# Gated attention with a mixture of experts on one core: when the values' banks are emptied, when Wk is turned, and where the sums for keys and values are made

## The chip, the cores and the metric

The kernel runs on one core of a Trainium2 chip. The core has TensorE (PE, matrix products), VectorE (DVE), ScalarE (ACT), GpSimd (POOL) and SyncE (SP, here only a queue that issues transfers). Each engine works off its own list of instructions in order; semaphores tie the lists together. The metric is the device time of one execution in microseconds, as the median of three runs.

## The reference

The input is `x`, 2 batches of 1024 tokens, 512 wide, all in float32. With `xn` the layer norm of `x`, the result is

```
qkv = xn @ w_qkv.T + b_qkv ;  q, k, v = split(qkv)
s   = softmax(q k' / sqrt(512)) v @ w_out.T + b_out
full_w = softmax weights of the 2 best of 8 experts, from xn @ router_w + router_b
f   = sum over experts e of full_w[e] * silu(xn @ expert_w[e] + expert_b[e])
y   = xn + f @ proj_w + proj_b
g   = silu(norm_w * y / rms(y))
out = x + s * g
```

## The kernel before, in words

The 2048 tokens are 16 tiles of 128 (`NT`). The kernel folds weights: the value and output weights become one matrix `rwvo`, the query and key weights one matrix `wqk`. So there is one product for the values and one for the queries, and the keys are the transposed tokens `xnT` themselves. The stages are:

1. **Weights** (to about 24 us): Wv, Wo and Wq are loaded; `wZ` is the buffer from which `turn_w` (line 132 on) transposes Wq, and later Wk, on DVE.
2. **Layer norm and values** (24 to 92 us, loop over `t` at line 442): `norm(g)` handles tiles 2g and 2g+1 in three parts. `stats` computes mean and variance on DVE and the root on ACT. `shifts` makes scale and shift on DVE. `rows` applies them on ACT, writes the tile to DRAM (`xn_d`), and, for tiles from 4 on, writes it a second time in blocks (`xn_s`) and reads it back (`xz`), from where `turn_x` transposes it on DVE into `xnT`. Tiles 0 to 3 are transposed on PE and copied by DVE (line 378). Each iteration multiplies one tile by `rwvo` (line 457) into a PSUM tile `pv` of the pool `ps_big`, which has two such tiles. ACT then copies the values to `vo` (line 465) and DVE adds the router's bias to the logits `lg1` (line 466). Only after both may the products of tile t+2 write that PSUM tile. Between the tiles lie the transposition of Wk, two weighted column sums (`sk`, `vb`), and at `t == 12` the load of all expert weights.
3. **Routing, queries and experts** (92 to 256 us): the tokens' order by expert, the product `wqk`, the queries of batch 0, and 39 blocks of expert products with their gathers. PE works there without a break.
4. **Attention** (256 us to the end), in pairs of tiles. The first pair's scores are made directly (`scores`, line 996). All later pairs use a scheme of Strassen and Winograd with 7 in place of 8 block products: `pair_scores` (line 1015) for scores, `attend` (line 1086) for probabilities times values. It needs sums of blocks of the right-hand factor, once for each batch: `right_sums` (line 866) makes t2, t3, t4 and overwrites block b12 by b12 - b11. `sum_right` makes them from the keys `xnT` on DVE, `sum_values` from the values `vo` on POOL, there in two halves for each sum. `sum_left` and `sum_p` make the sums for the left-hand factors on POOL. For each pair the expert outputs are gathered (`fetch`), scaled (ACT), combined (DVE), written to DRAM and read back in blocks (`cs`, `cz`), transposed (`turn_c`) and projected; `add_b` adds the projection's bias to the residual row `xr` on POOL. The probabilities take the same way through DRAM (`ps`, `pz`, `turn_p`).

What sets the order is the order in which the code is written: `keep_order` ties every instruction behind the one written before it for the same engine. So a step that waits holds up all that is written after it for that engine. The SP queue, too, takes its transfers strictly in that order, and each waits for the data that it moves and for the buffer that it fills. The part of the attention stage that precedes its loop is this, with the first batch's sums:

```
keys = sum_right(0)
next(keys)
sum_left(1)
both_of(fetch, 0)
sum_values(0)
scores(0)
...
*_, tw[0] = keys
```

`right_sums` is a generator: each `next` issues one sum. A product of pair 1 reads t2 first, then t3, b12, t4.

Of the kernel before, what the change touches and what calls it, by code (L numbers as in the profile page):

```python
# [14 lines left out]
ALU = mybir.AluOpType  # L15
# [5 lines left out]
P = 128  # L21
# [6 lines left out]
def kernel(  # L28
# [332 lines left out]
    def norm(g):  # L361
        stats(g)
        shifts(g)
        rows(g)
# [71 lines left out]
    direct(2)  # L436
    direct(3)
    norm(2)
    rows(1)


    for t in range(NT):
        if t % 2 == 0 and 0 < t and t + 6 < NT:
            norm(t // 2 + 3)
        if 3 < t < NT - 2:
            turn_x(t + 2)
        pv = ps_big.tile([P, 2, 512], FP, tag="big", name=f"pv{t}")
        for n, cols in ((1, ds(HH + E1, HH)), (0, ds(0, HH + E1))):
            if n == 0 and t in (1, 2):
                turn_x(t + 1)  # L450
            if n == 0 and t == 1:
                norm(3)
            if n == 0 and t == 3:
                turn_x(4)
                turn_x(5)
            for c in range(KC):
                pe.matmul(  # L457
                    pv[:, n, : HH + E1 * (1 - n)],
                    lhsT=xnT[t // ST][:, c, ts(t % ST, P)],
                    rhs=rwvo[:, c, cols],  # L460
                    start=(c == 0),
                    stop=(c == KC - 1),
                )
        dst = vo[t // ST][:, t % ST, :].rearrange("p (n f) -> p n f", n=2)
        act.copy(dst, pv[:, :, 0:HH])
        dve.tensor_tensor(lg1[:, t, :], pv[:, 0, HH : HH + E1], rb, ALU.add)
        if t == 1:
            spread(sp, wZ[1], w_qkvT[:, ts(1, H)])
        if t == 2:
            gps.dma_start(bo, b_out.partition_broadcast(P))  # L470
        if t == 4:
            turn_w(wqkT[:, KC:], wZ[1])
        if t == 6:
            sk_ = weighted(wqkT[:, KC:], bqk[:, 0], "sk")
        if t == 8:

            vb = weighted(wo, bqkv[:, 2], "vb")
        if t == 9:
            dve.tensor_copy(u, columns(sk_, "pu"))
        if t == 11:  # L480
            pvb = ps_mm.tile([P, 512], FP, tag="mm", name="pvb")
            pe.matmul(pvb, lhsT=ones, rhs=vb, start=True, stop=True)
            dve.tensor_tensor(bo, pvb, bo, ALU.add)
            close(raw_guard)
            ew_guard, ewp = pool("ew", side="right")
            ew = ewp.tile([P, E, KC, H], FP, name="ew")
        if t == 12:
            for e in range(E):
                sp.dma_start(ew[:, e], expert_w[e].rearrange("(c p) f -> p c f", p=P))
    close(ln_guard)  # L490
    eb_guard, ebp = pool("eb", side="right")
    eb = ebp.tile([P, E, H], FP, name="eb")
# [373 lines left out]
    def right_sums(b_, w_, eng, parts):  # L866

        b11, b12, b21, b22 = b_
        t2, t3, t4 = (w_[:, i] for i in range(3))
        def less(dst, l_, r_):  # L870
            for n in range(parts):
                c = ts(n, l_.shape[1] // parts)
                eng.tensor_tensor(dst[:, c], l_[:, c], r_[:, c], ALU.subtract)  # L873

        less(t3, b22, b12)
        yield
        less(b12, b12, b11)
        yield
        less(t2, b22, b12)
        yield  # L880
        less(t4, b21, t2)
        yield b12, t2, t3, t4

    def sum_right(b):
# [6 lines left out]
    def sum_values(b):  # L891
        if b == 0:
            w_ = at.tile([P, 3, SK, HH], FP, name="tv", bufs=1)
        else:

            w_ = keys_at[0][:, : 3 * SK * HH].rearrange("p (i k f) -> p i k f", i=3, k=SK)
        *_, tv[b] = right_sums(values(b), w_, gps, 2)

    def sum_p(k):

# [165 lines left out]
    def attend(k):  # L1066
# [53 lines left out]
        plus(c12, p5, c12)  # L1120
        yield
        p4 = times(a22, t4, ps_s, "s")
        finish(1, ds(HH, HH))
        plus(c21, p4, c21)
        yield
        if not last:
            plus(c12, times(s4, b22, ps_mm, "mm"), c12)
            for i in (1, 0):
                gate(rows[i], rows[i], two[i], ds(0, H))
                gps.tensor_tensor(rows[i], rows[i], base[two[i]], ALU.add)  # L1130
                sp.dma_start(out_d[:, two[i], :], rows[i])
        else:

            parts = [times(s4, b22[:, :, ts(n, P)], ps_mm, "mm") for n in range(2)]
            finish(1, ds(0, HH))
            finish(0, ds(HH, HH), store=False)
            for n in range(2):
                cols = ds(HH + n * P, P)
                gate(parts[n], parts[n], two[0], cols)
                plus(rows[0][:, cols], parts[n], rows[0][:, cols])  # L1140
                sp.dma_start(out_d[:, two[0], cols], rows[0][:, cols])
# [5 lines left out]
                step(t)  # L1147


    keys = sum_right(0)  # L1150
    next(keys)
    sum_left(1)
    both_of(fetch, 0)
    sum_values(0)
    scores(0)
    take_p(0)
    scores(1)
    close(ps_guard)
    ps_guard, ps_s = pool("ps_s", bufs=4, space=PSUM)
    *_, tw[0] = keys  # L1160
    both_of(scale_c, 0)
    both_of(inverse, 0)
    take_p(1)
    sp.dma_start(pb, proj_b.partition_broadcast(P))
    both_of(fetch_x, 0)
    both_of(combine, 0)
    both_of(take_c, 0)
    sp.dma_start(nw, norm_w.partition_broadcast(P))
    both_of(add_b, 0)
    both_of(fetch, 1)  # L1170
    queries_of(0, lambda name: ps_mm.tile([P, 512], FP, tag="mm", name=name))
    for k in range(NP):
        more = k + 1 < NP
        final = k + 2 == NP
        if more:
            n = pair_scores(k + 1)
            next(n)
            if k:
                both_of(scale_c, k + 1)
                both_of(turn_c, k)  # L1180
            if k + 1 == NPB:
                sum_values(1)
# [115 lines left out]
```

## Time and profile before

| what | value |
|---|---|
| median of three runs | 547.65 us (546.2, 547.65, 547.86) |
| the profiled execution's own time | 545.15 us |
| its span, first to last instruction | 543.5 us |
| PE busy | 527.6 us, 97% of the span |
| DVE busy | 315.8 us, 58% |
| ACT busy | 156.9 us, 29% |
| POOL busy | 225.0 us, 41% |
| mean granted clock of PE | 0.994 of full speed |
| the chain that ended last | PE 81%, DVE 8%, DMA 5% |

An instruction line of a timeline gives the start and the busy time in us, the engine, the line of the kernel, the operation, what is written and read, the shape, the count of instructions merged into it, and in brackets the idle time of the engine before it and what ended that. The line of a window gives its bounds and length, then busy time and count for PE, PE's weight loads, DVE, ACT and POOL, then PE's granted clock, the share of the transfer engines in use, and the rate in GB/s. The chain of waits gives start, duration and what the time was spent on, followed back from the last instruction to what released each one. PE's busy time counts a matmul as pipelined, so two neighbours overlap in it; the distance between starts is the true pace.

### The profile page before, as it was taken

The page shows a single profiled execution, that of the slowest core. Times are in us where ns is not written, and L with a number is a line of the kernel's source. Part 1 is how long each engine was busy: PE and PEld are TensorE (multiplying, and loading weights), DVE is VectorE, ACT ScalarE, POOL GpSimd, SP SyncE. Part 2 cuts the span into 40 slices and gives each one's busy share as a digit, 9 for nine tenths or more (in the row PEclk, how much of TensorE's full clock was granted, in tenths as well). Part 3 has the DMA queues.
Part 4 walks back from the last instruction along what each step waited for, and adds up shares of the span by engine and source line. Part 5 has one row for each costly group of instructions (what it writes and reads, how often), then busy time and mean ns, then how long its engine had stood idle before and what let it go on. Part 6 is the DMA issues. An engine that isn't in the chain of part 4 may idle for free.

```text
span 543.5 us, 5795 instructions
## 1 busy us (share of the span) xinstructions
PE 527.6 (97%) x1754; PEld 321.4 (59%) x1754; DVE 315.8 (58%) x525; ACT 156.9 (29%) x259; POOL 225.0 (41%) x239
## 2 busy tenths in 40 slices
PE   8969999999999999999989999999999999999996
PEld 7848787444444444444456666656756657484486
DVE  3645852831333333335498468376597685949686
ACT  3353322111211111112332522422425234152330
POOL 5000000023354863200777444346279855464542
PEclk9998999999999999999989999999999999999999
DMA  9879859839999999994556912822724728285512
GB/s 249 234 257 286 274 180 382 327 82 315 284 307 334 344 320 305 303 272 151 184 203 193 326 65 79 306 72 97 258 77 148 253 81 292 77 302 189 190 56 79
DMA packets 90928, 118.66 MB, mean 218 GB/s; under 512 B 6928, under 2 KB 55184, under 8 KB 90768
## 3 DMA queue, kind: packets, MB, share of 16 engines
q1 hardware_dynamic: 79344, 89.16, 51.1%
q0 software_dynamic: 5792, 18.88, 10.9%
q10 hardware_dynamic: 5760, 10.23, 5.0%
q8 instruction: 15, 0.25, 0.2%
q14 instruction: 17, 0.14, 0.1%
HBM read 73.69 MB, written 44.56 MB: 218 GB/s over the span
## 4 chain that ended last, share of the span: by engine, by line
PE 81%; DVE 8%; DMA 5%; issue 3%; ACT 1%; SPq 1%; DVEq 0%; ACTq 0%
PE ph L759 20%; PE so L1086 17%; PE pp L1015 14%; PE po L952 10%; PE pv L457 6%; PE pq L500 5%; PE pr L519 3%; PE sc L996 3%; PE pqk L531 3%; DMA wZ<-in_L_attn_w_qkv_dram 2%; DVE xnT L873 1%; DMA xn_d<-xn 1%; DMA xn_s<-xn 1%; DMA wo<-in_L_attn_w_out_dram 1%; DVE sc L1021 1%
## 5 line engine op out<-in xcount | busy, mean ns | idle before, releaser
L759 PE MATMUL ph<-ew,gT 128*128 x280 | 120.3, 592 | 0.0
L733 POOL DMA_INDIRECT xg<-xn_d,tok x39 | 37.3, 956 | 163.6 <-DVE npast L678 103.6
L759 PEld LDWEIGHTS ph<-ew,gT 128*128 128x128 f32 x280 | 53.2, 190 | 67.0 <-issue 67.0
L785 DVE TENSOR_TENSOR h<-ph,eb 128x512 f32<-128x512 f32 x39 | 26.8, 688 | 80.9 <-issue 53.1
L457 PE MATMUL pv<-rwvo,xnT 128*128 128x256 f32 (+1 forms) x256 | 60.2, 393 | 5.6 <-DVE xnT L378 5.0
L457 PEld LDWEIGHTS pv<-rwvo,xnT 128*128 128x128 f32 x256 | 48.9, 194 | 15.8 <-issue 4.2
L788 ACT ACTIVATE h<-h 128x512 f32<-128x512 f32 x39 | 24.6, 632 | 96.2 <-DVE h L785 87.8
L952 PE MATMUL po<-pw,ct 128*128 128x512 f32 x112 | 49.2, 592 | 0.0
L983 ACT ACTIVATE pr<-sc,nm 128x1024 f32<-128x1024 f32 x16 | 18.3, 1145 | 95.1 <-DVE nm L980 93.4
L1093 DVE TENSOR_TENSOR o<-so,o 128x256 f32<-128x256 f32 x49 | 20.0, 420 | 39.1 <-PE so L1086 22.2
L1130 POOL TENSOR_TENSOR o<-o,base 128x512 f32<-128x512 f32 x14 | 20.6, 1492 | 49.1 <-DVE o L1096 48.1
L1015 PE MATMUL pp<-xnT,qT 128*128 128x512 f32 x84 | 39.5, 592 | 0.0
L1086 PE MATMUL so<-vo,pT 128*128 128x256 f32 x168 | 38.5, 379 | 0.0
L952 PEld LDWEIGHTS po<-pw,ct 128*128 128x128 f32 x112 | 21.3, 190 | 25.5 <-issue 25.3
L1086 PEld LDWEIGHTS so<-vo,pT 128*128 128x128 f32 x168 | 31.9, 190 | 7.3 <-issue 2.6
L914 POOL DMA_INDIRECT hg<-ho_d,posi_m x32 | 31.4, 982 | 10.7 <-issue 6.7
L1021 DVE TENSOR_TENSOR sc<-pp,sc 128x512 f32<-128x512 f32 x49 | 31.6, 677 | 4.2 <-PE pp L1015 4.2
L120 DVE STREAM_TRANSPOSE gT<-sz 128x512 f32<-128x512 f32 x39 | 27.3, 700 | 7.3 <-DMA sz<-xs 7.3
L519 PE MATMUL pr<-xnT,wqk 128*128 128x256 f32 x128 | 28.8, 381 | 0.9 <-DVE sc L1021 0.9
L1015 PE MATMUL pp<-tw,sw 128*128 128x512 f32 x56 | 26.8, 623 | 2.5 <-DVE tw L873 2.5
L120 DVE STREAM_TRANSPOSE pT<-pz 128x1024 f32<-128x1024 f32 x14 | 28.1, 2008 | 0.0
L500 PE MATMUL pq<-xnT,wqk 128*128 128x512 f32 x64 | 28.1, 594 | 0.0
(210 smaller groups left out, 780.0 us busy)
## 6 DMA issues: line engine op xcount, KB each, us to landing
xs<-xg SPq DMA_DIRECT2D x39, 256.0 KB
sz<-xs SPq DMA_DIRECT2D x39, 256.0 KB
ho_d<-h ACTq DMA_DIRECT2D x39, 256.0 KB
ew<-in_L_ffn_expert_w_dram SPq DMA_DIRECT2D x8, 1024.0 KB
ps<-pr SPq DMA_DIRECT2D x16, 512.0 KB
pz<-ps SPq DMA_DIRECT2D x16, 512.0 KB
x<-_attn_hidden_states_dram SPq DMA_DIRECT2D x16, 256.0 KB
xn_d<-xn SPq DMA_DIRECT2D x16, 256.0 KB
```

Source lines behind the costliest of these rows:

```text
L120: dve.transpose(dst.rearrange(f"p j {order} -> p i j a", a=QP), z.rearrange("p i (j b) -> p i j b", b=QP),)
L457: pe.matmul(pv[:, n, : HH + E1 * (1 - n)], lhsT=xnT[t // ST][:, c, ts(t % ST, P)], rhs=rwvo[:, c, cols], start=(c == 0), stop=(c == KC - 1),)
L500: pe.matmul(ps[:, half, :], lhsT=wqk[:, c, ts(oc, P)], rhs=xnT[0][:, c, ts(half, 512)], start=(c == 0), stop=(c == KC - 1),)
L519: pe.matmul(ps[:, :PW], lhsT=wqk[:, c, ts(oc, P)], rhs=xnT[1][:, c, ts(k, PW)], start=(c == 0), stop=(c == KC - 1),)
L733: gps.indirect_dma_start(out=xg[s], out_offset=None, in_=xn_d, in_offset=bass.IndirectOffsetOnAxis(ap=tok[:, s : s + 1], axis=0),)
L759: pe.matmul(ph, lhsT=g_[:, c, :], rhs=ew[:, ds(r, 1), c, :].rearrange("p e f -> p (e f)"), start=(c == 0), stop=(c == KC - 1),)
L785: dve.tensor_tensor(h, ph, eb[:, ds(r, 1), :].rearrange("p e f -> p (e f)"), ALU.add)
L914: gps.indirect_dma_start(out=g_, out_offset=None, in_=ho_d, in_offset=bass.IndirectOffsetOnAxis(ap=posi_m[:, n, t : t + 1], axis=0),)
L952: pe.matmul(po, lhsT=c_[:, c, :], rhs=pw[:, c, :], start=(c == 0), stop=(c == KC - 1))
L1015: pe.matmul(ps, lhsT=l_[:, c, :], rhs=r_[:, c, :], start=(c == 0), stop=(c == KH - 1))
L1021: dve.tensor_tensor(dst, ps, other, ALU.add)
L1086: pe.matmul(ps[:, :w_], lhsT=l_[:, c, :], rhs=r_[:, c, :], start=(c == 0), stop=(c == SK - 1),)
```

## The change

In the layer-norm loop a tile's products (`value_side`) and the emptying of its PSUM tile (`keep_values`) become two functions, and iteration t empties tile t-1 after it has issued tile t's products. The layer norms of later tiles (`norm`, and `rows(1)`, which stood ahead of the loop) are written behind that, no longer ahead of the products. Wk's load goes from `t == 1` to `t == 4`, behind the transfers of tiles 10 and 11 in the SP queue, and its transposition from `t == 4` to `t == 8`; the sums that follow move by one to three iterations, and the closing of the buffers goes from `t == 11` to `t == 12`.

In `right_sums` t2 is now made as t3 + b11 in place of (b12 - b11) subtracted from b22, so t3, t2 and t4 all read only unchanged blocks, and b12 is overwritten last. The first batch's value sums are made on DVE, whole and not in halves (4 in place of 8 instructions); the second batch's stay on POOL. Ahead of the attention loop the sums are spread: two key sums before the first scores, one key sum and three value sums between the two scores, the overwriting of the keys' block behind the second softmax, and that of the values' block behind `combine`. The loads of `pb`, `xr` and `nw` and the `add_b` of the first pair go ahead of the scores, and the write of the combined rows goes ahead of the second read of probabilities. In the last `attend`, one `finish` moves ahead by one product.

```diff
-    rows(1)
...
     for t in range(NT):
-        if t % 2 == 0 and 0 < t and t + 6 < NT:
-            norm(t // 2 + 3)
         if 3 < t < NT - 2:
             turn_x(t + 2)
-        pv = ps_big.tile([P, 2, 512], FP, tag="big", name=f"pv{t}")
-        for n, cols in ((1, ds(HH + E1, HH)), (0, ds(0, HH + E1))):
-            if n == 0 and t in (1, 2):
-                turn_x(t + 1)
-            if n == 0 and t == 1:
-                norm(3)
-            if n == 0 and t == 3:
-                turn_x(4)
-                turn_x(5)
...
-        dst = vo[t // ST][:, t % ST, :].rearrange("p (n f) -> p n f", n=2)
-        act.copy(dst, pv[:, :, 0:HH])
-        dve.tensor_tensor(lg1[:, t, :], pv[:, 0, HH : HH + E1], rb, ALU.add)
+        value_side(t)
+        if t:
+            keep_values(t - 1)
         if t == 1:
-            spread(sp, wZ[1], w_qkvT[:, ts(1, H)])
+            rows(1)
+            norm(3)
+        if t == 3:
+            turn_x(4)
+            turn_x(5)
+        if t % 2 == 0 and 0 < t and t + 6 < NT:
+            norm(t // 2 + 3)
         if t == 2:
             gps.dma_start(bo, b_out.partition_broadcast(P))
         if t == 4:
+            spread(sp, wZ[1], w_qkvT[:, ts(1, H)])
+        if t == 8:
             turn_w(wqkT[:, KC:], wZ[1])
-        if t == 6:
+        if t == 9:
             sk_ = weighted(wqkT[:, KC:], bqk[:, 0], "sk")
-        if t == 8:
+        if t == 10:
             vb = weighted(wo, bqkv[:, 2], "vb")
-        if t == 9:
+        if t == 11:
             dve.tensor_copy(u, columns(sk_, "pu"))
-        if t == 11:
+        if t == 12:
             pvb = ps_mm.tile([P, 512], FP, tag="mm", name="pvb")
...
-        if t == 12:
             for e in range(E):
                 sp.dma_start(ew[:, e], expert_w[e].rearrange("(c p) f -> p c f", p=P))
+    keep_values(NT - 1)
...
         less(t3, b22, b12)
         yield
+        more(t2, t3, b11)
+        yield
+        less(t4, b21, t2)
+        yield
         less(b12, b12, b11)
-        yield
-        less(t2, b22, b12)
-        yield
-        less(t4, b21, t2)
         yield b12, t2, t3, t4
...
             w_ = at.tile([P, 3, SK, HH], FP, name="tv", bufs=1)
-        else:
-            w_ = keys_at[0][:, : 3 * SK * HH].rearrange("p (i k f) -> p i k f", i=3, k=SK)
-        *_, tv[b] = right_sums(values(b), w_, gps, 2)
+            return right_sums(values(b), w_, dve, 1)
+        w_ = keys_at[0][:, : 3 * SK * HH].rearrange("p (i k f) -> p i k f", i=3, k=SK)
+        return right_sums(values(b), w_, gps, 2)
...
         p4 = times(a22, t4, ps_s, "s")
+        finish(0, ds(HH, HH), store=False)
         finish(1, ds(HH, HH))
...
             finish(1, ds(0, HH))
-            finish(0, ds(HH, HH), store=False)
...
-    keys = sum_right(0)
-    next(keys)
+    keys, vals = sum_right(0), sum_values(0)
+    for _ in range(2):
+        next(keys)
     sum_left(1)
     both_of(fetch, 0)
-    sum_values(0)
+    sp.dma_start(pb, proj_b.partition_broadcast(P))
+    both_of(fetch_x, 0)
+    both_of(add_b, 0)
+    sp.dma_start(nw, norm_w.partition_broadcast(P))
     scores(0)
+    next(keys)
+    for _ in range(3):
+        next(vals)
     take_p(0)
     scores(1)
...
-    *_, tw[0] = keys
+    tw[0] = next(keys)
     both_of(scale_c, 0)
     both_of(inverse, 0)
+    both_of(combine, 0)
+    tv[0] = next(vals)
     take_p(1)
-    sp.dma_start(pb, proj_b.partition_broadcast(P))
-    both_of(fetch_x, 0)
-    both_of(combine, 0)
     both_of(take_c, 0)
-    sp.dma_start(nw, norm_w.partition_broadcast(P))
-    both_of(add_b, 0)
     both_of(fetch, 1)
...
             if k + 1 == NPB:
-                sum_values(1)
+                *_, tv[1] = sum_values(1)
```

More of the change, by code (lines that the diff above doesn't have):

```diff
@@ L438, with value_side @@
     norm(2)
-    rows(1)
-    for t in range(NT):
-        if t % 2 == 0 and 0 < t and t + 6 < NT:
-            norm(t // 2 + 3)
-        if 3 < t < NT - 2:
-            turn_x(t + 2)
+    pvs = {}
+    def value_side(t):
         pv = ps_big.tile([P, 2, 512], FP, tag="big", name=f"pv{t}")
+        pvs[t] = pv
         for n, cols in ((1, ds(HH + E1, HH)), (0, ds(0, HH + E1))):
@@ L463, with keep_values @@
                 )
+    def keep_values(t):
+        pv = pvs.pop(t)
         dst = vo[t // ST][:, t % ST, :].rearrange("p (n f) -> p n f", n=2)
@@ L466 @@
         dve.tensor_tensor(lg1[:, t, :], pv[:, 0, HH : HH + E1], rb, ALU.add)
-        if t == 1:
-            spread(sp, wZ[1], w_qkvT[:, ts(1, H)])
+    for t in range(NT):
+        if 3 < t < NT - 2:
+            turn_x(t + 2)
+        value_side(t)
+        if t:
+            keep_values(t - 1)
+        if t == 1:
+            rows(1)
[5 more added lines that the diff above has]
+            norm(t // 2 + 3)
         if t == 2:
@@ L869, in right_sums, with in_parts, less, more @@
         t2, t3, t4 = (w_[:, i] for i in range(3))
-        def less(dst, l_, r_):
+        def in_parts(dst, l_, r_, op):
             for n in range(parts):
                 c = ts(n, l_.shape[1] // parts)
-                eng.tensor_tensor(dst[:, c], l_[:, c], r_[:, c], ALU.subtract)
+                eng.tensor_tensor(dst[:, c], l_[:, c], r_[:, c], op)
+        def less(*which):
+            in_parts(*which, ALU.subtract)
+        def more(*which):
+            in_parts(*which, ALU.add)
         less(t3, b22, b12)
         yield
-        less(b12, b12, b11)
-        yield
-        less(t2, b22, b12)
+        more(t2, t3, b11)
         yield
         less(t4, b21, t2)
+        yield
+        less(b12, b12, b11)
         yield b12, t2, t3, t4
```

## The prediction

> **What bounds the kernel now.** I read the page first, then the chain of waits, then the timelines around each place where TensorE (PE) stands still, last the windows with the granted clock.
>
> ```profile
> PE   8969999999999999999989999999999999999996
> ...
> PEclk9998999999999999999989999999999999999999
> ```
>
> PE is busy 97% of the span. So only its few holes and slow stretches can be won: the 6 of slice 3 (27 to 41 us) and the 8 of slice 21 (272 to 285), with the clock's dips in slices 4 and 21. The chain of waits names what stands before PE there:
>
> ```profile
> 37.00 0.48 ACT vo L465
> ...
> 40.01 0.61 DVE xnT L378
> 40.76 5.45 PE pv L457 x16
> ...
> 77.53 14.06 PE pv L457 x64
> ...
> 271.80 7.96 DVE xnT L873
> ```
>
> A tile of values is 16 PE records. Unhindered it takes 14.06 / 4 = 3.51 us (last line but one); tile 3 took 5.45, 1.94 more. PE's timeline gives the holes:
>
> ```profile
> 33.21 1.97 PE L457 MATMUL pv<-rwvo,xnT 128*128 128x256 f32 x8 [1.67 <-DVE xnT L378]
> 40.76 19.50 PE L457 MATMUL pv<-rwvo,xnT 128*128 128x256 f32 x80 [3.36 <-DVE xnT L378]
> 60.78 7.58 PE L457 MATMUL pv<-rwvo,xnT 128*128 128x256 f32 x32 [0.52 <-DVE lg L466]
> ...
> 276.79 1.88 PE L1015 MATMUL pp<-xnT,qT 128*128 128x512 f32 x4
> 281.16 5.19 PE L1015 MATMUL pp<-tw,sw 128*128 128x512 f32 x8 [2.50 <-DVE tw L873]
> ```
>
> The first number in brackets is the hole. Behind two of them PE is slow, not just late; the windows (length, busy time by engine, then the granted clock) say why:
>
> ```profile
> 31.65:35.06 3.41, 1.85 (x9) 1.61 (x10) 2.33 (x7) 0.91 (x3) 0.00 (x0) 1.00 1.00 284
> 38.48:41.89 3.41, 1.13 (x5) 1.05 (x6) 1.71 (x6) 2.09 (x4) 0.00 (x0) 1.00 1.10 375
> 41.89:45.30 3.41, 3.41 (x9) 2.67 (x9) 2.08 (x3) 0.20 (x1) 0.00 (x0) 0.50 1.04 390
> 277.41:280.82 3.41, 1.25 (x3) 0.19 (x1) 3.38 (x2) 0.64 (x2) 1.26 (x2) 1.00 0.64 214
> 280.82:284.23 3.41, 3.07 (x4) 1.51 (x5) 3.38 (x6) 0.00 (x0) 1.52 (x2) 0.50 0.52 188
> ```
>
> After a window in which PE was busy 1.13 or 1.25 of 3.41 us the next ran at clock 0.50; after one with 1.85 it did not. DMA's share (last but one) is above 1 in the loop: transfers land there in the order of the queue, some 0.7 us apart.
>
> **Rule against row, the clock.** The Trainium skill (TensorE: Matmul & The Clock Gate, "What's actually happening") has the clock halved after an idle window of about 3.4 us. By it the 2.50 us hole costs 2.5. The row has 1.25 us of work in the window before and still 0.50 after: the 24 matmuls of pair 1 after the hole take 293.06 - 281.16 = 11.9 us where 24 x 0.43 = 10.3 would do, so the hole costs 2.5 + 1.6 = 4.1. I take the row, but the windows' place in a run is chance: a 2.5 us hole puts some 1.9 us into one window in about two of three positions.
>
> **The change, part by part: the loop.** Nothing is added; the orders on VectorE (DVE), ScalarE (ACT) and the SP queue move. A tile's bank is now emptied (ACT copy, then DVE's `lg` sum) behind the next tile's products. For even tiles that leaves ACT's order as it was (copy, layer norm's std and two xn, copy, copy); on DVE the transposed tiles now stand one place further ahead of `lg`. I replay it with durations of the trace. The layer-norm chain, from one `lg` (37.51) over statistics, std, shifts, two xn and the next copy to the next `lg` (42.12), is 4.6 us.
> - Tile 2. xn of tiles 2 and 3 (`rows(1)`) go behind copy 0, which runs at 30.3 and not 31.70. DVE's xnT of tile 2 goes before `lg`, done by 30.4. Tile 2 starts when tile 1 ends, 31.4, not 33.21.
> - Tile 3. xnT 3 now stands ahead of tile 4's statistics (done 34.4), which removes the releaser of the 3.36. But copy 1 is behind xn 7, which waits, as before, for a transfer that lands at 36.1 (xn 4's buffer). Copy 1 37.5, `lg` 37.7: start 37.75, not 40.76. This leaves a hole of 2.4, which may halve the clock of tile 3 (end 41.3, or 43.0).
> - Tile 4. Its turn on DVE waits for `lg` of tile 2, 42.3 by the 4.6 chain, plus 0.95: start 43.3 (46.24 before); the slow tile 3 is hidden by that wait.
> - Tile 5. DVE now has turns 5 and 6 ahead of `lg` 3, and turn 6 needs its transfer. The trace's record of landings has it at 46.6, and the SP queue up to there is unchanged. Turn 47.6, `lg` 47.75: start 47.8 (49.75 before), a new hole of 1.0.
> - Tile 6. The chain of 4.6 runs from that `lg`: 52.4 (53.25 before), a hole of 1.1.
> - After that PE is ahead of nothing: per two tiles it needs 7.0 us, the chain less. The four Wk transfers (42.99 to 44.55 issued, last landed 52.6, about 1.2 us each) have left the queue before xn 8's write, so turn 8 has its data at about 51.2 (needed 52.2), and go behind tile 11's; they land at about 61.5. DVE reaches `turn_w` (2.5) at 62.5, then the `sk` and `vb` sums (2.8 each) and three turns without a pause, so `lg` 9 is done at 70.05: 0.25 us of hole at tile 11. The hole of 0.52 and two of 0.27 in tiles 8 to 11 go.
> - End: 52.4 + 10 x 3.51 + 0.25 + two small products of 0.86 = 89.5, where the next product now starts at 91.5. **Gain 2.0**, although holes and slow clock were 8. The 8 MB of expert weights are issued 1.4 us later (79, not 77.56); they end near 110, gathers start near 113.
>
> **Keys and values.** DVE's view of the hole, with GpSimd's (POOL):
>
> ```profile
> 270.08 1.22 DVE L976 TENSOR_REDUCE nm<-sc 128x1 f32<-128x1024 f32 x1 [5.14 <-PE sc L996]
> ...
> 271.72 8.04 DVE L873 TENSOR_TENSOR xnT<-xnT 128x1024 f32<-128x1024 f32 x1
> 279.79 1.23 DVE L873 TENSOR_TENSOR tw<-xnT 128x1024 f32<-128x1024 f32 x1
> ```
>
> ```profile
> 264.10 0.96 POOL L914 DMA_INDIRECT hg<-ho_d,posi_m  x1 [1.01 <-DMA ho_d<-h]
> ...
> 268.82 2.50 POOL L873 TENSOR_TENSOR tv<-vo 128x512 f32<-128x512 f32 x2
> ...
> 276.19 2.48 POOL L873 TENSOR_TENSOR tv<-vo,tv 128x512 f32<-128x512 f32 x2
> ```
>
> An operation of 1.22 us took 8.04: it came to an end only when POOL's eight value sums did (278.67). Then two key sums followed and PE waited. In the change t3, t2 and t4 no longer read the changed block. t3 and t2 (2 x 1.23) fit between 260.49 and the first softmax at 263.21. t4 and three value sums (4 x 1.23 = 4.9) fill DVE's idle 5.14 before 270.08. The changed block comes after the second softmax, 271.8, behind whatever POOL then does. POOL loses eight sums (10 us) and gets `add_b` (1.5 + 1.7) from 269 on; its loads (pb, xr) are issued from about 256, when SP is idle. At worst DVE waits for it till 272.9 and has the block at 274.1. The product that needs it is the fourth of pair 1, at 276.79 + 3 x 1.72 = 281.9. The last value sum and two combines (5 us with contention) end before 280.3, DVE's first sum of pair 1. So the hole goes: pair 1 ends 28 x 0.43 = 12.0 after 276.79, at 288.8 and not 293.06. **Gain 4.2**. Later work follows: turn of the gathered tiles done at 294.5, wanted at 295.7; the sums of p on POOL end at 294, wanted at 302.6. The take of the second p moves behind two cs writes in SP, 277.2 as before.
>
> **Rule against row, the port.** By SBUF — State Buffer, "SBUF: two separate sides", a VectorE operation with two SBUF inputs and a GpSimd one exclude each other for one whole instruction. This speaks against the move: four DVE sums now lie beside the four gathers from 264.10. The 8.04 shows a longer hold, over the rest of a run of POOL instructions. The nearest row the other way round is this pair:
>
> ```profile
> 450.20 1.41 DVE L970 SCALAR_TENSOR_TENSOR y<-y,rrms,nw 128x512 f32<-128x512 f32 x2
> ...
> 450.97 1.46 POOL L914 DMA_INDIRECT hg<-ho_d,posi_m  x1 [0.30 <-issue]
> ```
>
> DVE ran on, the gather took 0.5 more. By that, gathers end about 1 us later; were they held for the whole run (till 269.9), they would end at 273.4 and land near 278, and the combine and last value sum would end at 280.4: 0.1 us of price. I take the row. The other way, DVE held by gathers and `add_b` (till 272), the second softmax would be 5 us late and PE's banks with it: 3 us of hole.
>
> **The rest.** Later batches' sums keep number and engine (POOL, 8 x 1.26, already there); only their order changes: nothing. In the tail one gate and sum (0.9 us) fills DVE's hole of 0.12 before 537.41: 0.1.
>
> **Sum.** 2.0 + 4.2 + 0.1 = 6.3 against the profiled 545.15 (span 543.5): 538.9. The runs' median, 547.65, is 2.5 above that execution. Halved clock behind the keys is met in two of three placements, so I count 1.1 of its 1.6: gain 5.7, **541.9**.
>
> **Rivals.**
> - Loop gives nothing (0.20). The transposed turns now wait in DVE ahead of `lg`; a transfer of tile 6 or 8 two us later shifts tile 6 by as much. For: queue full (share above 1). Against: tile 8's comes earlier. 543.9.
> - Keys give nothing (0.08): DVE held beside gathers and `add_b` as above, a 3 us hole in place of 2.5; 547.65 - 2.1 + 0.5 = 546.0.
> - Loop gives more (0.06): turn 6 has its data at 45.3, as 14 of its 16 parts did; tiles 5 and 6 follow without holes. 540.
> - Slower (0.08): `turn_w` waits in DVE for Wk, moved behind tile 11's transfers, and tile 12's queue behind it. Everything on DVE after 62.5 is late with it, one for one; 64.5 eats the loop's gain, 68.2 all of it. It takes transfers of 2.9 us in place of 1.2. At 71: 550.
> - The forecast (0.58), its own range 540.3 to 543.5.
>
> A measurement of this kernel tells 0.3% (1.6 us) from no change. Faster by more: 0.58 + 0.20 + 0.06 and a little of the second rival, 0.86; within it the rest of that, 0.06; slower 0.08. Range 539.2 to 545.4.
>
> **What would show it.** Right: PE's hole of 2.50 and its 0.50 window near 281 gone, DVE's changed block at 1.2 to 2.5 us; value tiles start near 31.4, 37.8, 43.3, 47.8, 52.4; DVE idle before turn 6 for its transfer. Wrong: a hole of PE in tiles 8 to 12 with DVE waiting for Wk; POOL's gathers stretched past 275; PE waiting for ct at the first projection.

## The result, and the profile after

| | before | after |
|---|---|---|
| median of 13 runs each, us | 546.2 (545.32 to 549.64) | 542.69 (540.4 to 545.93) |
| ratio, 95% interval | | 0.9935 (0.9913 to 0.9957) |
| profiled execution, us | 545.15 | 542.69 |
| its span, us | 543.5 | 541.0 |
| first value product to first `pqk` (the loop), us | 67.61 | 66.65 |
| first scores to first projection `po`, us | 43.83 | 41.69 |
| the rest, to the end | | the same within 0.1 |

The kernel became faster by 3.5 us (2.3 to 4.8 by the interval), 0.65%. The two profiled executions are only 2.46 us apart, and their stages add up: the loop gained 0.96, the keys' stage 2.14, and the loop began 0.67 later (24.49 and not 23.82) in this execution. That start is chance: the five kernels of this study that keep the loop of before, and so are the same up to there, began it between 23.82 and 27.30 us.

The busy share of PE in 40 slices of the span, and its granted clock, on the page of the kernel after:

```profile
PE   8979999999999999999999999999999999999996
...
PEclk9998999999999999999999999999999999999999
...
PE 74%; DMA 10%; DVE 8%; issue 4%; ACT 1%; POOL 1%; SPq 1%; DVEq 0%; POOLq 0%; ACTq 0%
```

The dip in slice 21 is gone, in work and in clock; the one in slices 3 and 4 is smaller, but there. In the chain that ended last (third line) DMA has risen to 10%, from 5%.

In the timeline of PE after, the two stages look like this:

```profile
39.55 5.47 PE L450 MATMUL pv<-rwvo,xnT 128*128 128x256 f32 x16 [3.40 <-DVE lg L462]
45.26 7.45 PE L450 MATMUL pv<-rwvo,xnT 128*128 128x256 f32 x32 [0.23 <-DVE xnT L120]
53.47 14.33 PE L450 MATMUL pv<-rwvo,xnT 128*128 128x256 f32 x64 [0.76 <-DVE lg L462]
...
284.12 1.98 PE L1033 MATMUL pp<-tw,qT 128*128 128x512 f32 x4 [0.60 <-ACT sc L1041]
...
293.98 3.72 PE L531 MATMUL pr<-xnT,wqk 128*128 128x256 f32 x16 [0.91 <-DVE sc L1039]
```

Tile 3 started at 39.55 and not at 37.75, behind a hole of 3.40; 0.67 of the difference is the later start of the loop. In place of the pause of 2.50 there were two, where I had forecast none: one of 0.60 us within pair 1's products and one of 0.91 in the products behind them. Why, the other engines show. VectorE, from the last expert blocks on:

```profile
261.58 0.69 DVE L797 TENSOR_TENSOR h<-ph,eb 128x512 f32<-128x512 f32 x1 [3.02 <-DMA ho_d<-h]
263.57 0.69 DVE L797 TENSOR_TENSOR h<-ph,eb 128x512 f32<-128x512 f32 x1 [1.30 <-DMA ho_d<-h]
264.18 1.22 DVE L885 TENSOR_TENSOR tw<-xnT 128x1024 f32<-128x1024 f32 x1
...
275.97 1.21 DVE L885 TENSOR_TENSOR xnT<-xnT 128x1024 f32<-128x1024 f32 x1
```

The changed block now takes 1.21 us, not 8.04. But the first key sum starts at 264.18, 3.7 us later than before (260.49), because two expert outputs `h` waited 3.02 and 1.30 us for earlier ones to be written out; before, that wait was 0.45. The chain of waits follows the same delay through POOL to the pause of PE:

```profile
256.26 5.20 DMA ho_d<-h
...
262.97 4.40 DMA ho_d<-h
...
267.58 0.73 POOL sw L872
...
278.30 4.56 DMA hg<-ho_d,posi_m
...
283.64 1.22 DVE vo L885
284.86 0.61 DVE sc L1039
```

The query sums start at 267.58 (258.99 before), the last gather at 278.30, and VectorE's first sum of pair 1 at 284.8, where I had put it at 280.3.

### The profile page after: what moved, and what is told of

It reads as the page before. It is cut to its first block, busy times and chain, and to the rows that moved or that the text cites. A ratio compares the mean times of both kernels' runs of the same rounds, so it can differ in the third digit from the quotient of the medians.

```text
span 541.0 us, 5784 instructions
## 1 busy us (share of the span) xinstructions
PE 527.2 (97%) x1754; PEld 320.9 (59%) x1754; DVE 314.9 (58%) x529; ACT 156.9 (29%) x259; POOL 217.7 (40%) x231
## 4 chain that ended last, share of the span: by engine, by line
PE 74%; DMA 10%; DVE 8%; issue 4%; ACT 1%; POOL 1%; SPq 1%; DVEq 0%; POOLq 0%; ACTq 0%
PE ph L771 20%; PE so L1104 17%; PE pp L1033 12%; PE po L970 10%; PE pq L512 5%; PE pv L450 4%; DMA wZ<-in_L_attn_w_qkv_dram 3%; PE pqk L543 3%; DMA xn_s<-xn 2%; PE pr L531 2%; DMA ho_d<-h 2%; DVE sc L1039 1%; DVE pT L120 1%; DMA xn_d<-xn 1%; DMA wo<-in_L_attn_w_out_dram 1%
## 5 line engine op out<-in xcount | busy, mean ns | idle before, releaser
L1001 ACT ACTIVATE pr<-sc,nm 128x1024 f32<-128x1024 f32 x16 | 18.3, 1146 | 89.5 <-DVE nm L998 78.4
L531 PEld LDWEIGHTS pr<-xnT,wqk 128*128 128x128 f32 x128 | 24.0, 190 | 8.1 <-DVE sc L1039 4.2
```

What stands on the lines that cost most here:

```text
L531: pe.matmul(ps[:, :PW], lhsT=wqk[:, c, ts(oc, P)], rhs=xnT[1][:, c, ts(k, PW)], start=(c == 0), stop=(c == KC - 1),)
```

## The experiments

All times are medians of runs beside runs of the kernel before. "Loop" and "keys" are the two distances of the table above, read in the profiled execution.

| kernel | us (runs) | ratio (95%) | loop | keys |
|---|---|---|---|---|
| before | 546.0 to 546.7 | 1 | 67.61 | 43.83 |
| loop alone | 544.6 (22) | 0.9971 (0.9956 to 0.9986) | 66.01 | 44.0 |
| keys alone | 544.1 (22) | 0.9964 (0.9946 to 0.9981) | 67.71 | 40.45 |
| after, loads put back | 540.99 (6) | 0.9906 (0.9878 to 0.9935) | 65.98 | 39.56 |
| before, loads moved | 542.02 (6) | 0.9921 (0.9891 to 0.995) | 68.28 | 39.56 |
| value sums behind the block | 542.32 (8) | 0.9939 (0.992 to 0.9959) | 67.57 | 39.56 |
| value sums whole on POOL | 542.42 (6) | 0.9938 (0.9916 to 0.996) | 67.58 | 39.56 |
| copy first | 540.47 (6) | 0.991 (0.9882 to 0.9939) | 66.27 | 39.57 |
| rows late | 542.22 (7) | 0.9928 (0.9897 to 0.9959) | 66.40 | 39.57 |
| loop, and whole sums | 541.43 (6) | 0.9911 (0.9881 to 0.9941) | 66.42 | 39.57 |
| rows late, Wk later | 537.46 (5) | 0.9854 (0.9834 to 0.9874) | 63.27 | 39.56 |

My theory after the result: the loop and the keys each give what was worked out, and what is missing went to the loads of `pb`, `xr` and `nw`, which now stand ahead of the last `h` writes. The rival: the loads are innocent, and the gathers and value sums hold each other up.

**The loop alone.** All of the change up to the expert stage (its core here), with the keys' part, the loads and the tail as before.

```diff
-        pv = ps_big.tile([P, 2, 512], FP, tag="big", name=f"pv{t}")
...
-        act.copy(dst, pv[:, :, 0:HH])
-        dve.tensor_tensor(lg1[:, t, :], pv[:, 0, HH : HH + E1], rb, ALU.add)
+        value_side(t)
+        if t:
+            keep_values(t - 1)
...
-        if t == 4:
+        if t == 8:
             turn_w(wqkT[:, KC:], wZ[1])
```

> The kernel before with the change's layer-norm loop alone (emptying one tile later, Wk loaded and turned later), keys and values untouched. Theory A (the loop's order is worth something, but each tile still waits for a transfer): value tiles 5 and 6 start some 1 to 2 us earlier than before, 1 us is left at the end of the loop, the hole of 2.5 us before pair 1 stays: 0.5 to 2 us faster than before. Rival (the changed kernel's whole gain lies here, the keys' part gives nothing): 3 to 3.5 us faster. Rival (loop gives nothing): within 0.5 us of before.

Measured 544.6, 1.4 us less by the medians and 1.6 by the ratio, with a loop of 66.01 (1.6 less) and the hole of 2.50 at the keys unchanged. So the loop's part works, at 1.0 to 1.6 us (the four executions with this code took 66.65, 66.01, 65.98 and 66.42) and not 2.0.

**The keys alone.** The keys' and values' sums and the loads as changed (cut here), with the loop and the tail as before.

```diff
+        more(t2, t3, b11)
+        yield
+        less(t4, b21, t2)
+        yield
         less(b12, b12, b11)
...
+            return right_sums(values(b), w_, dve, 1)
...
+    sp.dma_start(pb, proj_b.partition_broadcast(P))
+    both_of(fetch_x, 0)
+    both_of(add_b, 0)
+    sp.dma_start(nw, norm_w.partition_broadcast(P))
     scores(0)
```

> The kernel before with the change's keys and values part alone (order of the sums, first values' sums on VectorE, early loads of pb, xr and nw), loop untouched. Theory A (the hole before pair 1 goes, but the early loads cost a part of it again): 2 to 2.5 us faster, holes of about 0.6 and 0.9 us in pair 1 and behind it. Rival (no cost from the loads): 3.6 to 4.2 us faster. Rival (all from the loop): no change.

Measured 544.1, 1.9 us less. The hole before the keys' sums is gone, but a pause of 0.61 is left at the next products, and the stage takes 40.45, where 12.0 us of pair 1 without any pause would give 39.6.

**The loads put back.** The kernel after, with this one difference:

```diff
     both_of(fetch, 0)
-    sp.dma_start(pb, proj_b.partition_broadcast(P))
-    both_of(fetch_x, 0)
-    both_of(add_b, 0)
-    sp.dma_start(nw, norm_w.partition_broadcast(P))
     scores(0)
...
     take_p(1)
+    sp.dma_start(pb, proj_b.partition_broadcast(P))
+    both_of(fetch_x, 0)
     both_of(take_c, 0)
+    sp.dma_start(nw, norm_w.partition_broadcast(P))
+    both_of(add_b, 0)
```

> The changed kernel with the loads of pb, xr and nw and the first add_b back at their old place behind the second read of probabilities; all else as changed. Theory A (the loads stand ahead of the last expert blocks' writes in the transfer engines, and that is what delays VectorE's key sums by 3.7 us and the gathers by 9 us): the waits of h for its writes go, the first key sum starts near 260, gathers start near 264.5, pair 1 takes 12.0 us without a hole, and the time is 1.0 to 1.6 us below the changed kernel's. Rival B (VectorE's value sums and GpSimd hold each other up at the port, and that delays the gathers): gathers still start near 269 or later, the holes of 0.6 and 0.9 stay, time as the changed kernel's.

Measured 540.99, 1.7 below the kernel after. The intervals of the two ratios overlap, so what the loads cost is better read from the stage, which takes 39.56 and not 41.69: a gain of 4.27 over before, where 4.2 was forecast. VectorE's timeline of this kernel:

```profile
258.61 0.69 DVE L797 TENSOR_TENSOR h<-ph,eb 128x512 f32<-128x512 f32 x1 [0.45 <-DMA ho_d<-h]
...
276.42 1.22 DVE L885 TENSOR_TENSOR vo<-vo 128x1024 f32<-128x1024 f32 x1
```

The wait of `h` is 0.45 again, and the last value sum is issued at 276.42 instead of 283.64. The stage begins 0.97 us earlier here, so some 6 us of that are the loads' doing. PE has no pause in pair 1.

**The loads moved, and nothing else.** The kernel before, with the same loads of `pb`, `xr` and `nw` ahead of the first scores (`add_b` stays).

```diff
     both_of(fetch, 0)
+    sp.dma_start(pb, proj_b.partition_broadcast(P))
+    both_of(fetch_x, 0)
+    sp.dma_start(nw, norm_w.partition_broadcast(P))
     sum_values(0)
     scores(0)
...
     take_p(1)
-    sp.dma_start(pb, proj_b.partition_broadcast(P))
-    both_of(fetch_x, 0)
     both_of(combine, 0)
     both_of(take_c, 0)
-    sp.dma_start(nw, norm_w.partition_broadcast(P))
     both_of(add_b, 0)
```

> The kernel before with the four loads of pb, xr and nw moved ahead of the first scores and nothing else changed. Theory A: the last h on VectorE wait for their writes, the gathers start near 273 and not 264, GpSimd's value sums end near 288 and not 278.7, so that the hole before pair 1 grows from 2.5 to about 11 us: 7 to 10 us slower than before. Rival B (SP is idle there and the loads are free): within 0.5 us of before.

Measured 542.02: some 4 us faster, which neither theory had allowed. The delay of the `h` sums came as the first theory said, and here it can only be that of the loads, since `add_b` had not moved; the loss of time did not come. VectorE's timeline, and then GpSimd's:

```profile
265.88 0.69 DVE L785 TENSOR_TENSOR h<-ph,eb 128x512 f32<-128x512 f32 x1 [2.87 <-DMA ho_d<-h]
267.87 0.69 DVE L785 TENSOR_TENSOR h<-ph,eb 128x512 f32<-128x512 f32 x1 [1.30 <-DMA ho_d<-h]
...
275.87 1.21 DVE L873 TENSOR_TENSOR xnT<-xnT 128x1024 f32<-128x1024 f32 x1
...
278.38 2.17 DVE L873 TENSOR_TENSOR tw<-xnT,tw 128x1024 f32<-128x1024 f32 x1
```

```profile
272.87 0.97 POOL L914 DMA_INDIRECT hg<-ho_d,posi_m  x1 [6.60 <-DMA ho_d<-h]
...
277.93 3.75 POOL L873 TENSOR_TENSOR tv<-vo 128x512 f32<-128x512 f32 x2
```

The gathers waited 6.60 us for the late writes, so POOL's eight value sums began at 277.93, behind VectorE's changed block (275.87), which therefore took 1.21 us. A delay that costs the kernel after 2 us saved the kernel before 4: it took POOL's sums out of VectorE's way. That made a new theory: the whole loss of the keys' stage lies in the run of eight POOL sums that is under way when VectorE comes to its block. The next two kernels try it without touching a load.

**The value sums behind the block.** The kernel before, with the eight sums on POOL written later, and held there by a small operation that reads the keys' last sum:

```diff
-    sum_values(0)
     scores(0)
...
     *_, tw[0] = keys
+    late_ = cm.tile([P, 2], FP, name="late_", bufs=1)
+    gps.tensor_tensor(late_, tw[0][3][:, 0, 0:2], tw[0][3][:, 1, 510:512], ALU.subtract)
+    sum_values(0)
```

> The kernel before, with GpSimd's eight sums of the first values written behind the keys' sums and made to wait for their last one (one subtraction of two columns reads it). Theory A (the unbroken run of eight sums on GpSimd, 1.25 us each, is what stretches VectorE's changed block to 8.04 us and so makes the hole of 2.50 us): the block lasts 1.2 to 1.3 us, the keys' sums end about 275.7, the hole at the first pair products is below 0.2 us, the way from the first scores to the first value products falls from 43.8 to 39.6 us, GpSimd's sums lie at about 276 to 286, and the time is 3 to 4.5 us below before. Theory B (the hole has another cause: the late combines, or the loads in the transfer engines): the hole stays over 1.5 us and the time is within 1 us of before.

Measured 542.32, 3.8 us less than the 546.11 beside it, and the stage takes 39.56. VectorE's timeline, at the block and at the last of its sums:

```profile
271.99 1.22 DVE L873 TENSOR_TENSOR xnT<-xnT 128x1024 f32<-128x1024 f32 x1
...
274.50 1.23 DVE L873 TENSOR_TENSOR tw<-xnT,tw 128x1024 f32<-128x1024 f32 x1
```

Nothing else had to change: t2 still read the changed block, and the values were still summed on POOL, some 8 us later than before and in time for their product.

**The value sums whole on POOL.** The kernel before, with one digit changed:

```diff
-        *_, tv[b] = right_sums(values(b), w_, gps, 2)
+        *_, tv[b] = right_sums(values(b), w_, gps, 2 if b else 1)
```

> The kernel before, with the first values' four sums on GpSimd whole (four of 128x1024) instead of in halves (eight of 128x512), so that each needs the one before it and waits for it. Theory A (VectorE gets in between two GpSimd sums only where GpSimd itself waits, as it does in its query sums): the changed block lasts 2.0 to 4.0 us instead of 8.04, but the two sums after it wait for one GpSimd sum of about 2.5 us each, so the keys' sums end at about 281 to 283 as before and the time is within 1.5 us of before. Theory B (VectorE waits until GpSimd's queue of sums is empty, whatever its gaps): the changed block again lasts 7 us or more. Theory C (VectorE is let in after any GpSimd sum, and 8.04 us is something else): the block lasts under 2.0 us.

VectorE's timeline, then GpSimd's:

```profile
272.64 2.98 DVE L873 TENSOR_TENSOR xnT<-xnT 128x1024 f32<-128x1024 f32 x1
275.66 3.26 DVE L873 TENSOR_TENSOR tw<-xnT 128x1024 f32<-128x1024 f32 x1
278.96 3.26 DVE L873 TENSOR_TENSOR tw<-xnT,tw 128x1024 f32<-128x1024 f32 x1
```

```profile
272.19 2.36 POOL L873 TENSOR_TENSOR vo<-vo 128x1024 f32<-128x1024 f32 x1
274.63 3.22 POOL L873 TENSOR_TENSOR tv<-vo 128x1024 f32<-128x1024 f32 x1
```

The block took 2.98 us, the length that theory A gave: it ended some 1.1 us after the POOL sum during which it had been issued (272.19 + 2.36 = 274.55), and from there the two engines took turns. The Trainium skill (SBUF — State Buffer, "SBUF: two separate sides") has the two engines shut each other out for one whole instruction; this row fits that, the 8.04 us of before, over the rest of a POOL instruction and five whole ones, does not.

Theory A's reason is not shown, and other rows speak against it. Between two whole sums lies a pause of 0.08 us, in which POOL waits for its own last result; the half sums follow each other without one. But half sums without a pause have let VectorE in too. In the kernel with the loads moved (its lines are above) the keys' last sum, issued at 278.38 during the first half sum, ended at 280.55, and the first two half sums took 3.75 us instead of 2.50: VectorE ran between them. In the kernel before itself it got in between the half sums of the second batch: two combines, of 0.75 us each when alone, took 1.7 to 1.8, and two half sums 2.93. VectorE's timeline there, and GpSimd's:

```profile
400.42 3.44 DVE L928 SCALAR_TENSOR_TENSOR hg<-hg,wgt_m,hg 128x512 f32<-128x512 f32 x2
```

```profile
400.38 2.93 POOL L873 TENSOR_TENSOR xnT<-vo 128x512 f32<-128x512 f32 x2
```

So what keeps VectorE out for the rest of one half sum and five more in one place, and for one in another, is open. The long hold is no accident of one execution: the loop alone, which has the same code in this stage, shows 8.04 us again. What the runs show is that with whole sums, with later sums and with sums on VectorE the long hold is gone.

I was wrong on the time: 3.7 us faster (542.42 against 546.11) where I had said no change. The first product that waits is the one that reads t2, not t4. Here t2 was there at 278.92, 0.5 us before PE came to it at 279.43; before, it came at 281.02, 2.4 us behind the end of PE's product ahead of it.

**Copy first.** In the loop of the kernel with the loads put back, `norm(3)` (the rows of tiles 6 and 7) moves from `t == 1` to `t == 2`, behind the copy of tile 1.

> The kernel after with the loads of the earlier run back at their old place, and in the loop the rows of tiles 6 and 7 written one tile later, behind the emptying of tile 1's bank. Theory A (tile 3 starts late because the copy of tile 1 stands on ScalarE behind the row of tile 7, which waits for a store): tile 3 starts 2 to 3 us earlier than at 38.5, the loop takes 63.5 to 65.2 us instead of 66.0, and the time is 1 to 2.5 us below that of the loads put back alone (541.0), so 538.5 to 540. Theory B (the rows of tiles 6 to 8 come through memory no earlier, so the hole moves on to tiles 4 to 6): the loop stays at 65.6 us or more and the time at 540.5 to 541.5.

The hole moved on, as theory B said. ScalarE's timeline, and PE's:

```profile
32.89 0.56 ACT L461 COPY vo<-pv 128x512 f32<-128x512 f32 x1
...
41.87 0.81 ACT L333 ACTIVATE xn<-x,shift,rstd 128x512 f32<-128x512 f32 x1 [1.09 <-DMA xn_d<-xn]
42.59 1.05 ACT L461 COPY vo<-pv 128x512 f32<-128x512 f32 x2
```

```profile
44.49 2.04 PE L450 MATMUL pv<-rwvo,xnT 128*128 128x256 f32 x4 [4.77 <-DVE xnT L120]
```

Tile 3 now follows tile 2 without a hole, but the copy of tile 2 stands behind the rows of tiles 6 to 9 instead, till 42.59; the turn of tile 4 is behind it on VectorE, and PE waits 4.77 us in one place. But the cause given with theory B (the way through memory) is not what the trace shows: it is the order on ScalarE again, one tile later. The loop took 66.27, the time was 540.47, no different from the loads put back alone. Some 2 us of the 66.27 are the clock's, though: behind the long hole it was at 0.50 from 42.00 to 48.83, and PE worked for 4.3 us of that.

**Rows late.** So all later rows go behind the copy that they held up, and the turns behind it too. Against the kernel with the loads put back:

```diff
-        if 3 < t < NT - 2:
-            turn_x(t + 2)
         value_side(t)
...
-            norm(3)
+        if t == 2:
+            norm(3)
...
-        if t % 2 == 0 and 0 < t and t + 6 < NT:
-            norm(t // 2 + 3)
+        if 3 < t < NT - 2:
+            turn_x(t + 2)
+        if t % 2 == 1 and 1 < t and t + 5 < NT:
+            norm((t - 1) // 2 + 3)
```

> The kernel after with the loads of the earlier run back at their old place, and in the loop every later pair of rows (tiles 6 to 15) written one tile later, behind the emptying of the bank whose copy it held up, and each turn of a tile through memory behind that emptying too. Theory A (ScalarE's copies stand behind rows that wait for stores, and VectorE's bias sums behind turns that wait for their transfer; with both out of the way only the way through memory of tile 6 is left): tiles 3, 4 and 5 start at about 35, 39 and 43 and tile 6 at 48 to 50 instead of 52.4, the loop takes 62.5 to 64.5 us instead of 66.0, and the time is 537.5 to 539.5. Theory B (writing the rows later brings their tiles through memory later by as much): the loop stays at 65.6 us or more, and the time at 540 to 541.5.

The early part went as theory A said, the sum did not. PE's timeline:

```profile
40.16 3.75 PE L450 MATMUL pv<-rwvo,xnT 128*128 128x256 f32 x16 [1.24 <-DVE xnT L120]
45.48 17.84 PE L450 MATMUL pv<-rwvo,xnT 128*128 128x256 f32 x80 [1.56 <-DVE lg L462]
64.64 3.78 PE L450 MATMUL pv<-rwvo,xnT 128*128 128x256 f32 x16 [1.33 <-DVE lg L462]
70.70 3.78 PE L450 MATMUL pv<-rwvo,xnT 128*128 128x256 f32 x16 [2.28 <-DVE lg L462]
```

Tile 6 began at 49.1 where the kernel with the loads put back stood at 52.4, but two holes of 1.33 and 2.28 us (3.6 together) took it back; the loop takes 66.40. What VectorE did ahead of the first of them:

```profile
61.12 1.12 DVE L120 STREAM_TRANSPOSE xnT<-xz 128x512 f32<-128x512 f32 x1 [2.02 <-DMA xz<-xn_s]
62.07 2.46 DVE L134 STREAM_TRANSPOSE qT<-wZ 128x512 f32<-128x512 f32 x4
64.45 0.14 DVE L462 TENSOR_TENSOR lg<-pv,rb 128x9 f32<-128x9 f32 x1
```

A turn waits 2.02 us for its tile, then Wk is turned for 2.46, and only then comes the bias sum that frees PE's bank. Wk's four loads, issued at 48.3 to 50.7, now stood in SyncE's queue ahead of that tile's write.

**Rows late, Wk later.** The same kernel with Wk's load at `t == 6` (behind the fetches of tiles 10 and 11), its turn at `t == 10`, and what follows it two tiles later too.

```diff
-        if t == 4:
+        if t == 6:
             spread(sp, wZ[1], w_qkvT[:, ts(1, H)])
-        if t == 8:
+        if t == 10:
             turn_w(wqkT[:, KC:], wZ[1])
-        if t == 9:
+        if t == 11:
             sk_ = weighted(wqkT[:, KC:], bqk[:, 0], "sk")
...
```

> The kernel with the later rows and turns, with the loads of Wk two tiles later still (behind the fetches of tiles 10 and 11 in SyncE's queue) and its turn, the two weighted sums and what follows them, the experts' weights too, two tiles later. Theory A (in the later rows' kernel the 3.3 us won up to tile 6 are lost again because Wk's four transfers stand ahead of the way through memory of tiles 10 and 11, and its turn ahead of tile 8's bias sum): tile 10 starts at about 64 without the hole of 1.33 us before it, the hole of 2.28 us at tile 12 goes, the loop takes 63 to 64.5 us instead of 66.4, and the time is 537.5 to 539.5. Theory B (the tiles' way through memory is the limit wherever Wk stands, or the experts' weights are now late for the first expert product): the loop stays over 65.5 us, or a new hole opens at the first expert block, and the time is 540 or more.

Theory A held, to the end. PE's timeline:

```profile
46.55 25.11 PE L450 MATMUL pv<-rwvo,xnT 128*128 128x256 f32 x112 [1.56 <-DVE lg L462]
71.98 7.49 PE L450 MATMUL pv<-rwvo,xnT 128*128 128x256 f32 x32 [0.32 <-DVE lg L462]
```

112 matmuls run without a pause where there were 80, and the loop takes 63.27. No hole opens at the experts, though their weights are asked for later. At 537.46 us it is the fastest kernel of this study: 8.5 us below the 545.97 of before beside it, 0.9854 of its time.

**The loop, and whole sums.** The loop's part of the change, and of the keys' part only the digit.

```diff
-        *_, tv[b] = right_sums(values(b), w_, gps, 2)
+        *_, tv[b] = right_sums(values(b), w_, gps, 2 if b else 1)
```

> The loop's part of the change alone, and of the keys' part nothing but one digit: the first values' four sums whole on GpSimd instead of in halves. Theory A (the changed block's 8.04 us were the whole loss in the keys' stage, and it does not matter which engine makes the values' sums): the loop takes about 66.0 us, the way from the first scores to the first value products 39.6 us instead of 43.8, no hole at the first pair products, and the time is 540 to 541.5, about 2 us below the whole change. Theory B (the two gains share something, a start or a clock window, and don't add): above 542.

Measured 541.43, the keys' stage 39.57. So the gains add, and the edits on the keys (another formula for t2, the sums on VectorE, the new order) bring nothing over that digit in the length of the stage.

## Why the prediction was right and where it was wrong

The side was right, and 542.69 lies inside the range. The size was not: I forecast 5.7 us less, 0.9895 of the time before; the ratio is 0.9935 and its interval ends at 0.9913. That 542.69 lies so near to 541.9 is luck: the forecast was taken off 547.65, the median of three runs, and beside the kernel after the kernel before took 546.2.

- **Keys, the block: right.** I said that the hole comes from VectorE's block, held for the rest of POOL's run, and goes when the run goes. Four kernels that take POOL's run away from the block in four ways (sums on VectorE, sums late by accident, sums late on purpose, whole sums) all bring the stage to 39.6. The gain of 4.2, 2.5 of hole and 1.6 of halved clock, measured 4.27 with the loads put back. As a rule (a hold lasts for the rest of a run) it fails: see the half sums under the whole sums above.
- **Keys, the loads: the step that failed.** "its loads (pb, xr) are issued from about 256, when SP is idle" was counted as free. An idle queue says that nothing is in the way of the loads, not what the loads are in the way of. They are four transfers of 128 x 512 values, 1 MB in all, and the last `h` writes, issued by ACT in the same microseconds, landed late. The write issued at 256.26, 0.2 us after the load of `pb`, took 5.20 us; the seven last ones of the fastest kernel, which has the loads at their old place, took 2.0 in the median. I had listed what moves in SP's queue and left out what other queues had under way. The price was 4.27 - 2.14 = 2.1 us in the profiled execution; put back, the loads gave 1.7 by the medians. Only the load of `pb`, one row brought to all 128 partitions, stood ahead of that first slow write, and it took 4.7 us (the last number of this line of the kernel after's transfers, the time from issue to landing):

```profile
pb<-in_L_ffn_proj_b_dram SPq DMA_DIRECT2D x1, 256.0 KB, 4.7
```

  How much of the price is that of `pb`, and how much that of the two `xr` and of `nw`, is not separated: no kernel here moves one without the others. That the delay is in the transfer engines and not in the memory behind them was only argued.
- **Keys, the gathers beside VectorE's sums: small, as taken.** I weighed the port and put 0.1 us on it. In the kernel with the loads put back the gathers end at 271.2 beside four VectorE sums, one gather took 1.77 instead of 0.95, and PE has no pause.
- **Loop, up to tile 6: right in kind, tile 3 late by a transfer.** Copy 1 stands behind the row of tile 7, which waits until the row of tile 4 has been stored and its buffer is free. I took the landing of before, "lands at 36.1"; in the kernel after it was 37.91. The store was issued 8.13 us after the loop's first product in both, but landed 13.42 after it and not 12.27; in the three other executions with this loop it was 12.66 to 12.80. Why it came later is open. Counted from the first product, so that the later start drops out, tiles 3 to 6 began at 15.06, 20.77, 24.44 and 28.98, where 13.93, 19.48, 23.98 and 28.58 had been forecast; with the loads put back at 14.31, 20.00, 23.66 and 28.20. So up to tile 6 the loop brought what was forecast, within 0.4 us. (The starts given for tiles 4 to 6 before, 46.24, 49.75 and 53.25, are 0.2 late; PE's records have 46.04, 49.56 and 53.07.) The wait took 3.05 us of ScalarE, and the copy came right behind it:

```profile
38.02 0.81 ACT L333 ACTIVATE xn<-x,shift,rstd 128x512 f32<-128x512 f32 x1 [3.05 <-DMA xn_d<-xn]
38.73 0.56 ACT L461 COPY vo<-pv 128x512 f32<-128x512 f32 x1
```

- **Loop, turn 6 ahead of the bias sum of tile 3: right in kind.** VectorE idled 1.70 us for the transfer (till 47.75, forecast 46.6).
- **Loop, behind tile 6: the term that was mis-sized.** From tile 6 to the end I summed 37.1 us (89.5 - 52.4). It took 37.67 in the kernel after and 37.78 with the loads put back, 38.32 and 38.22 in the other two executions with this loop, and 38.36 before. That is where the loop fell short of its 2.0. A part is Wk: its four loads landed 1.0 to 1.7 us apart, the last at 64.32 and not 61.5, VectorE waited 0.52 us for them, and the bias sum behind the turn held up tile 10 by 0.19 us, by 0.29 to 0.84 in the other three. The rival in which that wait decides (71 needed for no gain at all) did not come; that Wk's place mattered all the same is shown by the kernels with late rows (66.40, and 63.27 with Wk later).
- **Rivals.** "Loop gives nothing" is refuted by the loop alone (0.9971, interval below 1). "Keys give nothing" is refuted by the keys alone (0.9964, interval below 1). "Loop gives more", with the data of turn 6 at 45.3, did not come: VectorE waited for them till 47.75. Half of the keys' gain was lost to a transfer, a case that I had only for the loop.

## What to carry to other kernels

When a load is moved to where its queue is idle, list what all the other queues have in flight at that moment and which engine waits for the last of it; a queue's idle time is no free capacity. Before work is moved to another engine because two engines exclude each other, try the cheap edits first: start one of them later, or cut its work into other pieces; a digit gave here what four moved sums gave, though why it did is open. And in a loop in which every engine works in order, emptying a bank should be written ahead of everything that may wait for memory: moved for one tile alone the hole only went to the next, and the full gain of 4.3 us came when rows, turns and the loads of Wk had all been put behind it.

## What the runs showed of the hardware that I had not expected

- **How long VectorE is held beside GpSimd differs by more than a factor of three for one kind of work.** The 128x1024 subtraction of two keys' blocks took 8.04 us beside a half sum of POOL and five more (in two executions), 2.17 where it ran between two such half sums, 2.98 and 3.26 beside whole sums 0.08 us apart, and 1.22 beside none. What decides is open. In the alternation POOL pays as well: 3.22 us for a whole sum, 2.36 alone.
- **Loads hold up writes of another queue by microseconds.** With the loads issued among the last `h` writes, two `h` sums waited 2.9 to 3.0 and 1.3 us for earlier writes in each of three kernels with that order; without them one waited, 0.45 us.
- **A hole in one place halves the clock in one execution and not in the next.** In the kernel after, a window with 0.39 us of PE work was followed by one at clock 0.50:

```profile
36.51:39.94 3.43, 0.39 (x2) 0.36 (x3) 0.61 (x2) 1.28 (x2) 0.00 (x0) 1.00 0.96 277
39.94:43.36 3.42, 3.42 (x10) 2.69 (x9) 1.43 (x6) 1.74 (x4) 0.00 (x0) 0.50 1.09 370
```

The hole there was of 3.40 us. With the loads put back, the same loop had holes of 2.64 and 1.91 us and kept its clock throughout; the kernel "loop, and whole sums" had one of 2.77 there, and the clock fell to 0.50 behind it. These loops took 66.65, 65.98 and 66.42 us in turn.
